# Gated delta rule: the next sequence's loading as steps of the second group's iteration, and the gate products ordered behind their neighbours on TensorE

## The chip, the cores and the metric

The kernel runs on one core of a Trainium2 chip. A core has a matrix engine (TensorE, PE in the profile; PEld is its loading of weights), a vector engine (VectorE, DVE), an engine for functions of one argument (ScalarE, ACT), a general engine (GpSimd, POOL) and one that issues transfers (SyncE, SP). Each works through a queue of its own, and they wait for one another by semaphores. The metric is the time of one execution on the device, in microseconds (us). The median of three runs before the change is 3416.7 us, from 3410.42 to 3425.55.

## The reference

The reference is a stack of four layers on 8 sequences of 512 tokens with 256 features, all in float32: a linear recurrence with an MLP, a mixture of experts, a gated delta rule, and attention over half of the tokens. The change touches the third layer. For each of 8 heads it computes

```python
beta = sigmoid(x @ Wb) * 2
g = -exp(A_log) * softplus(x @ Wa + dt_bias);  alpha = exp(g)
q = l2norm(silu(conv(x @ Wq)));  k = l2norm(silu(conv(x @ Wk)));  v = silu(conv(x @ Wv))

def step(state, inp):                      # over the tokens, state is 64 x 128 for a head
    retained = state @ k_t
    state = a_t * (state - b_t * outer(retained, k_t)) + b_t * outer(v_t, k_t)
    return state, state @ q_t

out = out * rsqrt(mean(out * out) + eps) * o_norm_w * silu(x @ Wg)
return out @ Wo
```

Its `x` is the layer norm of the sum of what came before, and its result is added to that sum. The sum includes the two experts' rows of each token, which lie in a buffer in memory in another order and are gathered when the sequence is loaded.

## The kernel before

`delta_rule` (from L566) takes a sequence's 512 tokens as 4 chunks of 128, and its 8 heads as 2 groups of 4. The recurrence inside a chunk is a triangular system, so that a chunk costs a few products and the inverse of a triangular matrix for each head. The loop at L1071 runs over 16 iterations `n`: sequence `n // 2`, group `n % 2`. An even `n` is called the first group's iteration here, an odd one the second group's.

The work of an iteration is written as generators, each step of which ends in a `yield`:

- `load` (L1016): brings a sequence's `x` in, gathers the rows of its experts eight times with POOL into two buffers `yg` and adds each with DVE (L1031, L1034), then normalises (`center`, L104, result `cz`), transposes (`turn`, L117: eight transposes into two PSUM banks `pc`, two copies by ACT into `cxT`), and calls `decays` (L632: products `pab` with `Wa` and `Wb`, a chain of small steps with Sigmoid, Exp and Ln on ACT, products `pdec`).
- `channels` (L671): the products `pc` for q, k and v, the convolution as one ACT copy and three DVE steps `cy` (L683, L685), Silu (L686).
- `norms` (L689) and `fade` (L721): the lengths of q and k, and the decays between the tokens of a chunk (`pe`, `e`).
- `prepare` (L736): the products `pk` of keys and queries inside a chunk, and from them `NQ`. It is the next group's.
- `inverses` (L751): the inverses for all 16 chunks and heads of the next group: `own` and `low` rearrange `NQ`, DVE inverts blocks of 16 (L789 to L817), and PE joins blocks of 16, 32 and 64 (`pn4`, `pd4`, `pu4`, `pn5` and so on), with ACT copying between the steps (`half`, `NQ`).
- `sides` (L896): transposes `ptv`, `ptk`. `silus` (L918): the gates' products `pg` (L924) and their Silu.
- `advance` (L930): the recurrence over the 4 chunks. From the second chunk on it goes `pkq` (PE, with the state), `old` and `r` (DVE, L952, L953), `pw` (PE), `w` (ACT, L959), `pst` (PE), `state` (DVE, L972), and beside it `pow` and the output `o`.
- `outputs` (L984): squares `oq`, their sum, the gates, transposes `pto`, products `py`, the addition to `x`, and after the second group the store.

The string `order` (L1059) says in which order the steps are written, one letter to a step. It isn't the order on the engines: a scheduler takes the traced instructions, and issues on each engine those that it reckons to be ready, with the written order as priority and the tiles' buffers as a limit. PSUM tiles come from four pools of two banks each: `pc` (`channels` and `turn`), `pa` (`decays`, `norms`, `fade`, `prepare`, `inverses`), `pt_` (`sides`, `silus`, `outputs`) and `pq` (`advance`). So a product can be issued early when its inputs are there and a bank is free. The lines that say when a sequence is loaded:

```python
if n + 2 < total:
    if n % 2 == 0:
        work["l"] = load(n // 2 + 1)
for k in order:
    if k in "cne" and n + 2 < total and k not in work:
        if "l" in work:
            drain(work["l"])
```

The channels of group `n + 2` need the loading, which is finished there whatever is left of it.

Of the kernel before, what the change touches and what calls it, by code (L numbers as in the profile page):

```python
# [14 lines left out]
F32 = mybir.dt.float32  # L15
# [5 lines left out]
P = 128  # L21
B, T, D = 8, 512, 256
NT = T // P
# [22 lines left out]
def block(ctx: ExitStack, tc: tile.TileContext, a: dict, out: bass.AP):  # L46
    nc = tc.nc
    V, S, G, TE = nc.vector, nc.scalar, nc.gpsimd, nc.tensor
# [68 lines left out]
    def turn(pool, tag, src, dst, n, weight=None):  # L117

        for c in range(DK):
            pt = pool.tile([P, T], F32, name=f"pt{n}_{c}", tag=tag)  # L120
            for t in range(NT):
                TE.transpose(pt[:, t * P : (t + 1) * P], src[:, t, c * P : (c + 1) * P], ident)
            if weight is None:
                S.copy(dst[:, c, :], pt)  # L124
            else:
                S.activation(dst[:, c, :], pt, AF.Copy, scale=weight[:, c : c + 1])
# [437 lines left out]


    def delta_rule():  # L566
        with ExitStack() as cx:
            wp = cx.enter_context(tc.tile_pool(name="c_w", bufs=1))
            wq = wp.tile([P, DK, H1 * P], F32, name="wq")
# [50 lines left out]
            tk = cx.enter_context(tc.tile_pool(name="c_tk", bufs=1))  # L620
# [3 lines left out]
            iv = cx.enter_context(tc.tile_pool(name="c_iv", bufs=1))  # L624
# [7 lines left out]
            def decays(b, xT):  # L632

                def s3(tag):
                    return sm.tile([P, NT, H1], F32, name=f"{tag}{b}", tag=tag, bufs=1 if tag.startswith("sp_") else 2)

                pab = pa.tile([P, NT, 2 * H1], F32, name=f"pab{b}", tag="pa")
                for t in range(NT):  # L640
                    for k in range(DK):
                        TE.matmul(pab[:, t, :], xT[:, k, t * P : (t + 1) * P], wab[:, k, :], start=k == 0, stop=k == DK - 1)
                beta = s3("beta")
                S.activation(beta, pab[:, :, H1:], AF.Sigmoid)
                V.tensor_scalar(beta, beta, 2.0, None, ALU.mult)


                y, e, u, l, d = s3("sp_y"), s3("sp_e"), s3("sp_u"), s3("sp_l"), s3("sp_d")
                V.tensor_add(y, pab[:, :, 0:H1], bc(dtb, 1, NT))
                V.scalar_tensor_tensor(e, y, -1.0, y, ALU.mult, ALU.max)  # L650
                S.activation(e, e, AF.Exp, scale=-1.0)
                V.tensor_scalar(u, e, 1.0, None, ALU.add)
                S.activation(l, u, AF.Ln)
                V.tensor_scalar(u, u, -1.0, None, ALU.add)
                V.tensor_scalar(d, u, 0.0, None, ALU.is_equal)
                V.tensor_add(u, u, d)
                V.tensor_add(l, l, d)
# [78 lines left out]
            def prepare(s):  # L736

                b, hg, kq = s.b, s.hg, s.kq
                NQ = s.NQ = hd.tile([P, 2, NU, P], F32, name=f"NQ{b}_{hg}", tag="NQ")
                for t in range(NT):  # L740
                    ts = slice(t * P, (t + 1) * P)
                    e = s.es[t]
                    for h in range(0, HG, 2):
                        pk = pa.tile([P, 2, 2, P], F32, name=f"pk{b}_{hg}_{t}_{h}", tag="pa")
                        for j in range(2):
                            TE.matmul(pk[:, j, :, :], kq[:, h + j, 0, ts], kq[:, h + j, :, ts], start=True, stop=True)  # L746
                        for j in range(2):
                            V.scalar_tensor_tensor(NQ[:, :, t * HG + h + j, :], pk[:, j, :, :], s.nbk[:, t, h + j : h + j + 1], bc(e[:, h + j, :], 1, 2), ALU.mult, ALU.mult)  # L748
                        yield

            def inverses(s):  # L751
# [3 lines left out]
                nm, N = f"{s.b}_{s.hg}", s.NQ[:, 0, :, :]  # L755
# [17 lines left out]
                for a_ in range(4):  # L773
                    q = slice(32 * a_, 32 * a_ + 32)
                    o = own[q, :, :].rearrange("p j (h n) -> p j h n", h=2)
# [3 lines left out]
                V.scalar_tensor_tensor(L[:, 0:256].rearrange("p (r c) -> p r c", c=16), low[:, :, 0:16], front, low[:, :, 16:32], ALU.mult, ALU.add)  # L779
                yield  # L780

                def tmp(what, shape, bufs=2):
                    n = math.prod(shape)
                    t = iv.tile([P, 512], F32, name=f"{what}{nm}", tag="tmp", bufs=bufs)[:, 0:n]
                    names = "abc"[: len(shape)]
                    return t.rearrange(f"p ({' '.join(names)}) -> p {' '.join(names)}", **dict(zip(names, shape)))

# [228 lines left out]
            def load(b):  # L1016

                q = SimpleNamespace(b=b)
                seqs[b] = q
                x = q.x = tk.tile([P, NT, D], F32, name=f"cx{b}", tag="x", bufs=2)  # L1020
                nc.sync.dma_start(x, rows_of(xbufs[0][b]))
                late = []
                for t in range(NT):
                    for j in range(2):
                        at = b * NT + t
                        yg = un.tile([P, D], F32, name=f"yg{b}_{t}_{j}", tag="yg", bufs=2)
                        G.indirect_dma_start(yg, None, ybuf, bass.IndirectOffsetOnAxis(ap=rows[j][:, at : at + 1], axis=0))  # L1027
                        late.append((t, yg, wts[j][:, at : at + 1]))
                        if len(late) > 1:
                            u, y, w = late.pop(0)  # L1030
                            V.scalar_tensor_tensor(x[:, u, :], y, w, x[:, u, :], ALU.mult, ALU.add)  # L1031
                        yield
                for u, y, w in late:
                    V.scalar_tensor_tensor(x[:, u, :], y, w, x[:, u, :], ALU.mult, ALU.add)  # L1034
                yield
                z = tk.tile([P, NT, D], F32, name=f"cz{b}", tag="z")
                center(sm, x, z, f"c{b}")
                yield
                q.xT = tk.tile([P, DK, T], F32, name=f"cxT{b}", tag="xT", bufs=2)
                turn(pc, "pc", z, q.xT, f"c{b}")  # L1040
                q.g, q.beta, q.dec = decays(b, q.xT)
                yield

# [5 lines left out]
            def drain(*work):  # L1049
                for w in work:  # L1050
                    for _ in w:
                        pass
# [2 lines left out]

            order = """  # L1059
                p v p v p l a v p l a v p l a l p a l p a l p a l p l a i a l l g a i l l c g i a a e i a g i e c i a a i e g e  # L1060
                i o c i o c o i c o i c i o o c i i c o i i c o n o n c c n
            """.split()
            groups = {}
            drain(load(0))
            total = B * (H1 // HG)
            for n in range(2):
                s = groups[n] = group(n)
                drain(channels(s), norms(s), fade(s))
                if n == 0:
                    drain(prepare(s), inverses(s))  # L1070
            for n in range(total):  # L1071
                s, s1 = groups.pop(n), groups.get(n + 1)
                work = {"v": sides(s), "g": silus(s), "a": advance(s), "o": outputs(s)}
                if s1 is not None:
                    work |= {"p": prepare(s1), "i": inverses(s1)}
                if n + 2 < total:
                    if n % 2 == 0:
                        work["l"] = load(n // 2 + 1)
                for k in order:
                    if k in "cne" and n + 2 < total and k not in work:  # L1080
                        if "l" in work:
                            drain(work["l"])
                        if n + 2 not in groups:
                            groups[n + 2] = group(n + 2)
                        work[k] = {"c": channels, "n": norms, "e": fade}[k](groups[n + 2])
                    if k in work:
                        next(work[k], None)
                drain(*work.values())

    delta_rule()  # L1090


# [292 lines left out]
```

## Time and profile before

| | |
|---|---|
| median of three runs | 3416.7 us |
| the profiled execution, its own time | 3412.4 us |
| its span, first to last instruction | 3410.6 us |
| PE / DVE / ACT / POOL busy | 89% / 55% / 45% / 19% |
| mean granted clock of TensorE | 0.912 |
| delta rule, first to last transposition or addition of `cx` | about 1544 to 2940 us |

The profile is of one execution. A line of a timeline has the start, the length, the engine, the line of the kernel, the operation, what is written and read, how many instructions stand together, and in brackets the idle time before it and who ended it. A float32 product counts as two PE instructions. The ends of products are modelled. A line of waits has who waited for whom, the total, how often, and the longest. The granted clock is TensorE's share of full speed: at 0.5 a product takes twice as long and still counts as busy.

### The profile page before, as it was taken

What the parts mean: (1) busy time and instruction counts of PE and PEld (TensorE: products, weight loads), DVE (VectorE), ACT (ScalarE), POOL (GpSimd) and SP (SyncE); (2) the same over time, 40 slices, a digit from 0 to 9 for tenths busy, and PEclk for the clock granted to TensorE, in tenths of its full rate; (3) what the DMA queues carried; (4) which work ended last, traced back from release to release, by engine and by line L of the source; (5) the groups of instructions that cost most, each with busy time, mean ns of one, the idle gap of its engine ahead of it and who ended that gap; (6) DMA issues with size and microseconds to landing.
All of it is one profiled execution on the core that took longest, in us unless ns stands there. A gap on an engine that the chain in (4) does not pass through costs nothing. (4 is left out here: it accounts for less than half of the span.)

```text
span 3410.6 us, 59501 instructions
## 1 busy us (share of the span) xinstructions
PE 3049.4 (89%) x24662; PEld 2239.6 (66%) x24662; DVE 1871.4 (55%) x4375; ACT 1528.4 (45%) x2735; POOL 636.5 (19%) x669
## 2 busy tenths in 40 slices
PE   7999999889999999977898999999999998488887
PEld 3655655445999999973666666666666667366564
DVE  4555545334555555546466666666666665554432
ACT  3554442112333333335465757575756565233322
POOL 1000003441011000113131313132222220112111
PEclk8999998999999999998788989899989898687787
DMA  5000003210688888870000000000000000201111
GB/s 204 13 25 13 13 13 147 68 66 19 247 332 329 336 326 318 330 278 20 2 2 26 2 26 2 26 2 26 2 26 2 23 2 8 87 28 38 38 41 47
DMA packets 97133, 302.69 MB, mean 89 GB/s; under 512 B 12760, under 2 KB 79456, under 8 KB 87648
## 3 DMA queue, kind: packets, MB, share of 16 engines
q0 software_dynamic: 19440, 221.19, 17.3%
q1 hardware_dynamic: 68016, 68.44, 6.0%
q10 hardware_dynamic: 9408, 9.27, 0.8%
q8 instruction: 194, 3.18, 0.4%
q14 instruction: 75, 0.61, 0.1%
HBM read 248.79 MB, written 50.08 MB: 88 GB/s over the span
## 5 line engine op out<-in xcount | busy, mean ns | idle before, releaser
L444 PE MATMUL p_r<-zT,w 128*128 128x128 f32 x4544 | 532.8, 275 | 6.8 <-DMA w<-in_experts,wrow 5.6
L444 PEld LDWEIGHTS p_r<-zT,w 128*128 128x128 f32 x4544 | 525.0, 192 | 12.1 <-issue 6.7
L685 DVE SCALAR_TENSOR_TENSOR cy<-pc,conv,cy 128x511 f32<-128x511 f32 (+2 forms) x480 | 353.0, 741 | 99.0 <-ACT cy L683 93.9
L448 ACT ACTIVATE t_r<-p_r,w 128x128 f32<-128x128 f32 x568 | 171.0, 374 | 262.9 <-PE p_r L444 175.8
L444 PE MATMUL p_s<-sxT,shared_w 128*128 128x512 f32 x512 | 224.1, 598 | 1.7 <-ACT sxT L124 1.7
L444 PEld LDWEIGHTS p_s<-sxT,shared_w 128*128 128x128 f32 x512 | 97.4, 192 | 122.6 <-issue 109.2
L449 DVE SCALAR_TENSOR_TENSOR l_r<-p_r,w,t_r 128x128 f32<-128x128 f32 x284 | 80.0, 344 | 175.6 <-PE p_r L444 175.6
L508 POOL DMA_INDIRECT w<-in_experts,wrow x71 | 66.9, 943 | 576.9 <-ACT sg_r L457 565.6
L681 PE MATMUL pc<-cxT,wk 128*128 128x512 f32 x256 | 153.0, 715 | 11.0 <-DVE cy L685 7.6
L681 PE MATMUL pc<-cxT,wq 128*128 128x512 f32 x256 | 147.5, 692 | 6.7 <-DVE cy L685 4.2
L304 PE MATMUL pp<-hT,win 128*128 128x512 f32 x320 | 143.1, 599 | 0.1
L522 PE MATMUL pyr<-w,htr 128*128 128x256 f32 x568 | 135.3, 381 | 2.9 <-DVE htr L462 2.9
L449 DVE SCALAR_TENSOR_TENSOR g_r<-p_r,w,t_r 128x128 f32<-128x128 f32 x284 | 80.0, 345 | 98.1 <-PE p_r L444 98.1
L683 ACT ACTIVATE cy<-pc,conv 128x512 f32<-128x512 f32 x160 | 108.5, 685 | 52.1 <-PE pc L681 51.2
L748 DVE SCALAR_TENSOR_TENSOR NQ<-pk,nbk,e 128x256 f32<-128x256 f32 x256 | 108.8, 478 | 31.6 <-PE pk L746 30.6
L746 PE MATMUL pk<-kq 128*128 128x256 f32 x512 | 125.7, 384 | 0.4 <-DVE NQ L748 0.4
L1027 POOL DMA_INDIRECT yg<-ybuf,rows x64 | 63.2, 987 | 314.6 <-DVE cx L1031 281.7
L394 PE MATMUL pf<-hT,fc 128*128 128x512 f32 x256 | 121.6, 602 | 0.0
L457 ACT ACTIVATE sg_r<-g_r 128x512 f32<-128x512 f32 x71 | 44.8, 630 | 160.1 <-DVE g_r L455 160.1
L399 PE MATMUL pj<-pj,sT 128*128 128x256 f32 x512 | 113.1, 379 | 0.0
L522 PEld LDWEIGHTS pyr<-w,htr 128*128 128x128 f32 x568 | 102.8, 191 | 14.3 <-issue 2.7
L950 PEld LDWEIGHTS pkq<-state,kq 128*128 128x128 f32 x768 | 103.9, 212 | 6.1 <-issue 3.3
(393 smaller groups left out, 6226.9 us busy)
## 6 DMA issues: line engine op xcount, KB each, us to landing
zt<-zbuf SPq DMA_DIRECT2D x71, 128.0 KB
ybuf<-yt SPq DMA_DIRECT2D x71, 128.0 KB, 3.2
zbuf<-zeros SPq DMA_DIRECT2D x11, 768.0 KB, 10.7
x<-in_x SPq DMA_DIRECT2D x8, 512.0 KB
xbuf<-x SPq DMA_DIRECT2D x8, 512.0 KB, 2.9
sx<-xbuf SPq DMA_DIRECT2D x8, 512.0 KB, 4.0
xbuf<-sx SPq DMA_DIRECT2D x8, 512.0 KB, 2.9
cx<-xbuf SPq DMA_DIRECT2D x8, 512.0 KB, 3.8
```

Source lines behind the costliest of these rows:

```text
L304: TE.matmul(ps, win[:, k, m : m + P], hT[:, k, :], start=k == 0, stop=k == DK - 1)
L394: TE.matmul(ps, fc[:, k, f * P : (f + 1) * P], hT2[:, k, :], start=k == 0, stop=k == DK - 1)
L399: TE.matmul(ps, sT[:, f, t * P : (t + 1) * P], pj[:, f, :], start=f == 0, stop=f == 7)
L444: last_of[0] = TE.matmul(ps[:, f, :], wx[:, k, (f0 + f) * P : (f0 + f + 1) * P], xin[:, k, :], start=k == 0, stop=k == DK - 1)
L448: S.activation(t3[:, f, :], p3[:, f, :], AF.Identity, bias=b3[:, f0 + f : f0 + f + 1])
L449: V.scalar_tensor_tensor(t1[:, f, :], p1[:, f, :], b1[:, f0 + f : f0 + f + 1], t3[:, f, :], ALU.add, ALU.mult)
L522: last_of[0] = TE.matmul(ps, hT[:, f, :], w2[:, f, :], start=f == 0, stop=f == 3)
L681: TE.matmul(ps, w[:, k, n * P : (n + 1) * P], xT[:, k, :], start=k == 0, stop=k == DK - 1)
L683: S.activation(y, ps, AF.Copy, scale=conv[:, at + n, 3:4])
L685: V.scalar_tensor_tensor(y[:, j:], ps[:, : T - j], conv[:, at + n, 3 - j : 4 - j], y[:, j:], ALU.mult, ALU.add)
L746: TE.matmul(pk[:, j, :, :], kq[:, h + j, 0, ts], kq[:, h + j, :, ts], start=True, stop=True)
L748: V.scalar_tensor_tensor(NQ[:, :, t * HG + h + j, :], pk[:, j, :, :], s.nbk[:, t, h + j : h + j + 1], bc(e[:, h + j, :], 1, 2), ALU.mult, ...
```

## The change

The loading starts one iteration earlier, as work of the second group's iteration, in ten steps (`l`): eight gathers, the last addition, and `center`. The last two steps (`t`), `turn` and `decays`, which are now separate, follow early in the first group's iteration after it. Ten steps of sequence 1 are done ahead of the loop. For that `x` gets three buffers for two, and `cz` takes the buffer of `oq` (tag `oq`) for one of its own. The order string is rewritten round these letters. And the gates' products are put behind the last product written before them: `Queue` keeps the last TensorE instruction that `delta_rule` writes itself, and `tc.issue_after` adds an order on the same engine, without a wait for completion. `turn` lies outside and goes on with the engine itself. In `tmp` (L782) a parameter that nobody set is dropped.

```diff
+        class Queue:
+            def matmul(self, *args, **kw):
+                self.last = nc.tensor.matmul(*args, **kw)
+            def transpose(self, *args, **kw):
+                self.last = nc.tensor.transpose(*args, **kw)
+        TE = Queue()
...
-                x = q.x = tk.tile([P, NT, D], F32, name=f"cx{b}", tag="x", bufs=2)
+                x = q.x = tk.tile([P, NT, D], F32, name=f"cx{b}", tag="x", bufs=3)
...
-                z = tk.tile([P, NT, D], F32, name=f"cz{b}", tag="z")
+                z = tk.tile([P, NT, D], F32, name=f"cz{b}", tag="oq")
                 center(sm, x, z, f"c{b}")
                 yield
                 q.xT = tk.tile([P, DK, T], F32, name=f"cxT{b}", tag="xT", bufs=2)
                 turn(pc, "pc", z, q.xT, f"c{b}")
+                yield
                 q.g, q.beta, q.dec = decays(b, q.xT)
                 yield
...
             order = """
-                p v p v p l a v p l a v p l a l p a l p a l p a l p l a i a l l g a i l l c g i a a e i a g i e c i a a i e g e
-                i o c i o c o i c o i c i o o c i i c o i i c o n o n c c n
+                p v t p v p l a v p t l a v p a p a p l a p a p a i l a i g a i c l g i a a e i l a g i e c i a a i l e g e
+                i c o i l c o c i o c i l c o i o c i o l i c o i i c o n o n c c n
             """.split()
...
+            coming = load(1)
+            for _ in range(10):
+                next(coming)
             for n in range(total):
...
-                if n + 2 < total:
-                    if n % 2 == 0:
-                        work["l"] = load(n // 2 + 1)
+                if n % 2 == 0 and coming is not None:
+                    work["t"] = coming
+                elif n + 3 < total:
+                    work["l"] = coming = load(n // 2 + 2)
+                else:
+                    coming = None
                 for k in order:
                     if k in "cne" and n + 2 < total and k not in work:
-                        if "l" in work:
-                            drain(work["l"])
+                        if "t" in work:
+                            drain(work["t"])
...
-                    if k in work:
+                    if k == "g":
+                        with tc.issue_after(TE.last.ins):
+                            next(work[k], None)
+                    elif k in work:
                         next(work[k], None)
+                work.pop("l", None)
                 drain(*work.values())
```

More of the change, by code (lines that the diff above doesn't have):

```diff
@@ L780, in inverses, with tmp @@
                 yield
-                def tmp(what, shape, bufs=2):
+                def tmp(what, shape):
                     n = math.prod(shape)
-                    t = iv.tile([P, 512], F32, name=f"{what}{nm}", tag="tmp", bufs=bufs)[:, 0:n]
+                    t = iv.tile([P, 512], F32, name=f"{what}{nm}", tag="tmp")[:, 0:n]
                     names = "abc"[: len(shape)]
```

## The prediction

> **What bounds the kernel now.** I read the page first. TensorE (PE) is busy 89% and is the last engine to wait almost everywhere; the chain that ended last covers under 1% of the span and says nothing here. The change touches the delta rule only, from about 1540 to 2940 us.
>
> ```profile
> PE 3049.4 (89%) x24662; PEld 2239.6 (66%) x24662; DVE 1871.4 (55%) x4375; ACT 1528.4 (45%) x2735; POOL 636.5 (19%) x669
> ```
>
> Next the stretches from one first `pw` product to the next: one per iteration, a sequence's first head group (long), then its second (short). After the length come the busy time and count of PE, PEld, DVE, ACT and POOL, then the granted clock.
>
> ```profile
> 1993.50:2087.90 94.40, 84.88 (x937) 60.30 (x935) 60.29 (x141) 57.66 (x87) 23.57 (x24) 0.89 0.07 20
> 2087.90:2160.70 72.80, 69.11 (x877) 50.42 (x874) 51.23 (x105) 49.23 (x74) 16.58 (x16) 0.95 0.02 6
> ...
> 2327.80:2419.00 91.20, 81.70 (x937) 57.80 (x935) 60.51 (x141) 57.80 (x87) 23.73 (x24) 0.93 0.07 21
> 2491.80:2591.70 99.90, 87.54 (x936) 61.65 (x934) 60.91 (x141) 57.96 (x87) 23.47 (x24) 0.86 0.07 19
> ...
> sum 1010.20, PE 926.88 PEld 664.43 DVE 669.93 ACT 642.10 POOL 239.72; mean PE 77.24 PEld 55.37 DVE 55.83 ACT 53.51 POOL 19.98
> ```
>
> Six sequences take 1010.2, so 168.4 each. Sequence 2 takes 167.2: PE idle 9.5 + 3.7 = 13.2, busy 154.0. The clock column shows 94.4 x 0.11 + 72.8 x 0.05 = 14 us of clock withheld, some 2 of it in idle time, so about 12 of the busy time is slow clock and 142 is work at full clock. The waits of PE over these six sequences name the idle time:
>
> ```profile
> PE pw L957 <- DVE r L953: 23.7, 6, 4.2
> PE pd L837 <- ACT oms L994: 16.1, 6, 2.7
> PE pow L976 <- ACT w L959: 7.6, 12, 0.8
> ```
>
> One wait of some 4 us and one of 2.7 per sequence. Their price is larger than their length. PE's timeline round the first:
>
> ```profile
> 2015.27 1.89 PE L950 MATMUL pkq<-state,kq 128*128 128x64 f32 x16
> 2021.22 1.86 PE L957 MATMUL pw<-r,NQ 128*128 128x64 f32 x8 [4.05 <-DVE r L953]
> ...
> 2027.07 3.62 PE L950 MATMUL pkq<-state,kq 128*128 128x64 f32 x16
> ```
>
> The same `pkq` takes 1.89 before and 3.62 after: stretches of 3.4 us show a clock of 0.50 from 2023.6 to 2040.6. DVE's timeline tells why `r` was late; adds of the load that wait for a gather, and the inverse's transpose, stand ahead of `old` and `r`:
>
> ```profile
> 2015.58 0.48 DVE L1031 SCALAR_TENSOR_TENSOR cx<-yg,wts,cx 128x256 f32<-128x256 f32 x1 [1.86 <-DMA yg<-ybuf,rows]
> ...
> 2017.28 0.71 DVE L763 STREAM_TRANSPOSE low<-own 128x512 f32<-128x512 f32 x1 [0.48 <-ACT own L776]
> ...
> 2019.11 0.68 DVE L952 TENSOR_TENSOR old<-pkq,dec 128x512 f32<-128x512 f32 x1
> 2020.25 0.49 DVE L1034 SCALAR_TENSOR_TENSOR cx<-yg,wts,cx 128x256 f32<-128x256 f32 x1 [0.46 <-DMA yg<-ybuf,rows]
> 2020.65 0.42 DVE L953 TENSOR_TENSOR r<-r,old 128x256 f32<-128x256 f32 x1
> ```
>
> Last, ACT's switches between function tables (count, total, mean ns):
>
> ```profile
> L686 ACT ACT_TABLE_LOAD x6 | 7.7, 1283 | 3.5 <-issue 2.8 <-DVE cy L685 0.7
> L731 ACT ACT_TABLE_LOAD x5 | 6.4, 1283 | 0.1
> ```
>
> **What the Trainium skill says.** "TensorE: Matmul & The Clock Gate", Part 1: a window of about 3.4 us without work halves PE's clock, and a busy window restores it. The trace agrees on 0.50, but a gap of 2.68 us, less than a window, is enough here. "ScalarE: Activation LUTs", What ACT_TABLE_LOAD costs: 1283 ns and a drain of 1380. The 1283 is in the rows; of the drain I see nothing, since after the load that ends at 2052.71 `dec` starts at 2052.73. "Perfetto Trace Analysis", Tensor Engine Instruction: DVE, ACT and POOL are strict FIFO. The DVE lines show it: `old` needs no gather and waits behind one.
>
> **The change part by part.** No computing instruction goes or comes; orders and waits do. I use the orders in which both built programs stand, and walk them with the durations above.
>
> *Loading.* As written, it spreads over the second group's iteration. As ordered, it doesn't: with a third `x` the scheduler draws the eight gathers and adds back into the first group's recurrence, one sequence further ahead. What leaves the recurrence is `center`'s last step (4 x 0.40 of DVE), the eight transposes (1.92 at half clock) and two copies (1.07 of ACT) of `turn`; they stand at the second group's end, 1.0 of PE at full clock. The gathers land 2.8 us after issue; about 7 us of DVE work lies between the add that frees a buffer and the next use, so I price their waits at 0.3 a sequence. If that cover goes, `old` and `r` wait again as now, up to 4 us. On SP, the load of `x` waits for the store of three sequences before, which ends in the same iteration as today's; store and load land in 2.9 and 3.8, and the first add comes some 8 us later. Nothing. The scheduler's choice is thus already a part of the claim that fails.
>
> *`cz` in `oq`'s buffer.* It waits for the reduction of `oq` (1.2) that precedes it in DVE's order; the next `oq` comes a whole recurrence later. Nothing on PE; but four `cz` (1.6) now delay the gates in the second group: about 1 us late for `pto`.
>
> *`pg` after its written neighbour.* Two tiles (4 products, 1.7 us) stand between the second `pkq` and `pw`, two round the third. DVE needs 0.68 + 0.41 there: the 4.05 is covered, if nothing else is ahead. The edge is order alone; gates are read only after the recurrence.
>
> *`decays` as a step of its own, early.* `pab` now precedes the first `pkq` and the first `pc` products become filler. Its chain of Sigmoid, Exp and Ln took from 2038.2 to 2050.3; now it runs inside the recurrence. At step 1, `r` stands behind one more `cy` (0.68 + 0.74 + 0.41 = 1.8 against one `pc` of 0.86): 1.0 idle. The Ln load (1.28) holds a DVE step and `state` behind it: 0.8. Also `pab` and `pdec` take the two `pa` banks, so the last products of `prepare` come after `pdec`, and the inverse chain starts one recurrence step late.
>
> *What is late next.* From the end of the last `pkq` DVE needs `old` 0.68, `L` 0.64, `r` 0.41, seven small rows with statistics 3.9, `o` 0.42, four steps 1.04 + 0.69 + 1.08 + 0.68, `both` 0.68, then `cols` 0.61 on ACT and `dn` 0.71: about 11. PE has 7 queued before `pn4`: 4.1 idle. Then `half` waits behind `oq` 1.04, two copies 1.4, a Sqrt load 1.28, `rsc` and `oms`: 3.5. Sequences 2, 4, 6 come so. Sequences 1, 3, 5 stand in another order: 19 loads in the first group's iteration (13 before), 7 in the second's (10 before). There `w` of step 1 waits for the Ln load (1.6) and the tail for six more loads, 7.7 us; I make its idle time 10.4.
>
> Sum, even sequences: 142 work + 1.0 + 0.8 + 0.3 + 4.1 + 3.5 + 2.9 (two `half`-fed waits after) + slow clock over some 12 us, 4, + second group 2.4 idle and 2 slow = 163. Odd: 142 + 0.3 + 1.6 + 10.4 + 1.5 + 8 slow + 1.9 = 165.7. Mean 164.4 against 168.4: 4.0 less. The first and last sequences have parts of it, so 6.5 x 4.0 = 26. The profiled execution of 3412.4 becomes 3386. It lies 4.3 below the median of 3416.7; on that scale I say 3391.
>
> **Unknown sizes.** Slow clock: none at all would save 5 more a sequence, and lasting to the iteration's end costs 5. Tail waits: from 0 if ACT gets ahead of its queue, to 18 if every load lands on the path. A gain is possible too, since filler hides late inputs.
>
> **Rivals.** (1) *The late inverse sets the end: slower.* One step of the recurrence is about 10 us, and all of it may be exposed between the last `pow` and `pn5`. For: DVE and ACT are in order, and the filler has been moved ahead. Against: `pc` tiles can still be interleaved. My sums have 9 of idle time there; break-even is 13 (9 + 4.0), and at 18.5 a sequence takes 5.5 more than now: 3416.7 + 36 = 3453. (2) *PE stays at full clock: much faster.* For: 12 us of slow clock a sequence come from two waits that both get filler. If the tail waits halve too, a sequence takes 154: 6.5 x 14.4 = 94, so 3323. Against: the tail has no filler left. (3) *An exchange:* the wait at `pw` reappears at `pn4` at the same price, 3400 to 3434. For: the same work on DVE and ACT must precede it.
>
> **How the numbers follow.** Forecast 0.36 (own range 3370 to 3400), rival 1 0.26, rival 2 0.18, rival 3 0.20. About 0.5%, 17 us, is what a measurement tells here. Faster takes the forecast and rival 2: 0.54; rival 3 is the same, 0.20; slower 0.26. Rival 2 covers 3300 to 3365 and rival 1 3434 to 3480; the range 3328 to 3462 leaves out the outer parts of both, 0.09 and 0.08.
>
> **What would show it.** Right: `pw` no longer waits 4 us for `r`; `pn` of the first inverse product waits for `dn` by 3 to 5 us in first-group iterations, and `pn5` for `half`; the half clock moves from the recurrence to the tail; odd sequences are longer in the first group; 20 and 26 table loads a sequence against 23. Wrong: waits for gathers on DVE ahead of `old` again, clock at 0.5 in the recurrence, or tail waits over 13 us.

## The result and the profile after

The changed kernel takes 3392.1 us (median of 4 runs, 3391.5 to 3397.4) against 3421.1 for the kernel before on the same chip (four runs, of which the prediction's 3416.7 is the median of three): a ratio of 0.992, with a 95% interval of 0.989 to 0.995. It is faster by 0.8%. The profiled execution took 3392.6 us with a span of 3390.8, and the one before 3412.4 with 3410.6.

First the line of busy times, where ACT's count has gone from 2735 to 2745, all of them table loads:

```profile
PE 3014.9 (89%) x24662; PEld 2225.2 (66%) x24662; DVE 1896.5 (56%) x4375; ACT 1541.7 (45%) x2745; POOL 632.6 (19%) x669
```

Next the stretches from one first `pw` to the next, as before the change (length, busy time and count of PE, PEld, DVE, ACT, POOL, then granted clock): sequence 2 with its two groups, sequence 3 with its two, and the six sequences from 1 to 6 together:

```profile
2002.90:2092.70 89.80, 79.43 (x933) 58.00 (x932) 64.03 (x141) 58.60 (x87) 25.17 (x24) 0.92 0.06 19
2092.70:2162.00 69.30, 67.61 (x894) 49.62 (x893) 53.35 (x109) 46.95 (x73) 16.44 (x16) 1.00 0.04 12
2162.00:2256.20 94.20, 80.10 (x916) 58.50 (x915) 62.80 (x136) 63.93 (x90) 23.66 (x24) 0.86 0.05 16
2256.20:2329.90 73.70, 68.25 (x878) 49.35 (x877) 52.44 (x105) 45.03 (x70) 15.50 (x16) 0.95 0.03 8
1837.70:2815.60 977.90, 882.28 (x10815) 645.01 (x10814) 687.81 (x1439) 645.71 (x959) 229.52 (x230) 0.92 0.04 12
```

A sequence takes 163.0 on average (977.9 / 6) and took 168.4. Two forms alternate: sequences 2, 4 and 6 take 159.1, 160.7 and 157.7, sequences 1, 3 and 5 take 165.2, 167.9 and 167.3. The waits of PE over the same six sequences (who waited for whom, total, times, longest):

```profile
PE pn L571 <- ACT e L741: 21.2, 4, 6.0
PE pu L571 <- issue: 14.4, 10, 2.4
PE pn L571 <- DVE dn L773: 6.9, 2, 3.7
...
PE pw L571 <- DVE inv L804: 6.2, 2, 3.1
PE pw L571 <- DVE r L963: 5.8, 13, 0.9
```

The wait of `pw` for `r`, 4.2 at its longest before, is at most 0.9. In its place `pn`, the first product of the inverses (`pn4`), waits up to 6.0. The waits of `pu` named "issue" are 14.4 in all, 4.0 before; the profile shows nothing that ended them, and what they are is open. Most of the half clock has moved to the tail too, but not all: in sequences 1, 3 and 5 it is 0.50 for 3.4 to 6.8 us in the second recurrence step, after a wait of 1.37 of `pst` for `w`. PE's timeline from the last `pw` of sequence 2's first group into its tail, and the product `pn4` in sequence 3:

```profile
2044.76 1.07 PE L571 MATMUL pw<-r,NQ 128*128 128x64 f32 x8 [3.12 <-DVE inv L804]
...
2055.13 1.32 PE L571 MATMUL pn<-dn,NQ 32*32 32x16 f32 x128 [3.67 <-DVE dn L773]
...
2062.70 0.49 PE L571 MATMUL pn<-half,NQ 32*32 32x32 f32 x8 [1.51 <-ACT half L849]
2063.13 2.07 PE L571 MATMUL pc<-cxT,wq 128*128 128x512 f32 x2
```

```profile
2214.72 1.91 PE L571 MATMUL pn<-dn,NQ 32*32 32x16 f32 x128 [5.98 <-ACT e L741]
```

Two `pc` instructions take 2.07 in sequence 2's tail, where four took 1.94 at full clock just before (at 2049.53). In sequence 3 `dn` was written by 2213.50; the wait's last 1.2 us are for ACT's `e`, which reads `pe` in one of the two `pa` banks and had come behind a table load (1.28).

Where the time went, then. The first `pw` of the delta rule comes at 1670.0 and came at 1662.5; sequence 0 takes 167.7 and took 163.0; sequences 1 to 6 are 32.3 shorter together; what follows takes 575.2 (3390.8 - 2815.6) and took 574.9. 7.5 + 4.7 - 32.3 + 0.3 = -19.8, the difference of the spans.

### The profile page after: what moved, and what is told of

Read it like the earlier page. It is cut to its first block, busy times and chain, and to the rows that moved or that the text cites. A ratio compares the mean times of both kernels' runs of the same rounds, so it can differ in the third digit from the quotient of the medians.

```text
span 3390.8 us, 59551 instructions
## 1 busy us (share of the span) xinstructions
PE 3014.9 (89%) x24662; PEld 2225.2 (66%) x24662; DVE 1896.5 (56%) x4375; ACT 1541.7 (45%) x2745; POOL 632.6 (19%) x669
## 5 line engine op out<-in xcount | busy, mean ns | idle before, releaser
L444 PEld LDWEIGHTS p_r<-zT,w 128*128 128x128 f32 x4544 | 526.9, 192 | 11.8 <-issue 6.1
L695 DVE SCALAR_TENSOR_TENSOR cy<-pc,conv,cy 128x509 f32<-128x509 f32 (+2 forms) x480 | 351.4, 740 | 120.9 <-ACT cy L693 116.1
L571 PE MATMUL pc<-cxT,wq 128*128 128x512 f32 x256 | 143.8, 682 | 14.4 <-DVE cy L695 10.9
L571 PE MATMUL pc<-cxT,wk 128*128 128x512 f32 x256 | 143.6, 654 | 7.2 <-DVE sp_l L669 3.3
L738 POOL TENSOR_TENSOR e<-le,g 128x512 f32<-128x512 f32 x64 | 68.3, 1073 | 351.9 <-DVE NQ L758 314.6
```

The costliest lines, as they stand in the source:

```text
L444: last_of[0] = TE.matmul(ps[:, f, :], wx[:, k, (f0 + f) * P : (f0 + f + 1) * P], xin[:, k, :], start=k == 0, stop=k == DK - 1)
L571: self.last = nc.tensor.matmul(*args, **kw)
L695: V.scalar_tensor_tensor(y[:, j:], ps[:, : T - j], conv[:, at + n, 3 - j : 4 - j], y[:, j:], ALU.mult, ALU.add)
L738: G.tensor_mul(e, bc(le, 1, HG), bc(s.g[:, t, hs], 2, P))
```

## The experiments

All times below are per sequence from sequence 1 to 6, first `pw` to first `pw`, in the profiled execution; the ratio is that of the medians to the kernel before on the same chip. Idle is PE's time without work. "Half" is PE's busy time in stretches whose granted clock is 0.5, so half of it is lost; "work" is the rest, the busy time less half of "half".

| kernel | median us | ratio (95%) | a sequence | idle | half | work |
|---|---|---|---|---|---|---|
| before | 3421.1 | 1 | 168.4 | 13.9 | 26.2 | 141.4 |
| changed | 3392.1 | 0.992 (0.989 to 0.995) | 163.0 | 15.9 | 18.2 | 137.9 |
| e1 edge alone | 3458.9 | 1.014 (1.009 to 1.019) | 175.1 | 16.3 | 37.2 | 140.2 |
| e2 no edge | 3391.6 | 0.993 (0.991 to 0.996) | 161.2 | 15.3 | 17.5 | 137.1 |
| e3 sequence 1 written later | 3406.5 | 0.997 (0.995 to 0.999) | 162.0 | 16.1 | 16.3 | 137.7 |
| e4 decays in other banks | 3397.9 | 0.994 (0.992 to 0.995) | 164.2 | 12.8 | 23.2 | 139.9 |
| e5 sequence 2 held | 3391.7 | 0.992 (0.989 to 0.994) | 162.4 | 15.1 | 18.2 | 138.2 |
| e6 as e4, `pdec` later | 3337.4 | 0.975 (0.972 to 0.978) | 154.8 | 10.1 | 13.5 | 137.9 |
| e7 before, no gathers | 3380.4 | 0.988 (0.985 to 0.992) | 167.2 | 11.8 | 30.7 | 140.0 |
| e8 decays late | 3339.2 | 0.977 (0.974 to 0.980) | 153.4 | 8.8 | 10.6 | 139.3 |
| e9 as e8, no edge | 3372.6 | 0.985 (0.982 to 0.989) | 160.3 | 12.1 | 20.1 | 138.1 |
| e10 as e8, sequence 2 held | 3337.2 | 0.975 (0.971 to 0.978) | 153.7 | 9.8 | 9.3 | 139.2 |
| e11 as e8, channels held | 3422.6 | 1.003 (1.001 to 1.004) | 168.3 | 12.0 | 33.4 | 139.7 |
| e12 as e8, no gathers | 3290.2 | 0.963 (0.958 to 0.968) | 149.8 | 6.8 | 7.6 | 139.2 |

The work is 137 to 141 in all fourteen, so what differs is idle time and slow clock. The spread of 4 in that column says how finely this division can be read.

### The two halves of the change apart: e1 and e2

e1 is the kernel before with `Queue` and the edge only:

```diff
+                    if k == "g":
+                        with tc.issue_after(TE.last.ins):
+                            next(work[k], None)
-                    if k in work:
+                    elif k in work:
```

> The kernel before with only the gates' products queued behind the last product written before them; loading, order string and buffers stay. Theory (the loading's place and the early decays make the gain, the edge itself little): the adds of the gathers still stand ahead of `old` and `r` on DVE in the third recurrence step, so `pw` still waits some 4 us for `r`, the half clock after it stays, a sequence stays at 168 +- 1.5, the time within 0.5% of before. Rival (the gates' products are what fills the wait): `pw` waits under 1.5 us there, a sequence takes 163 to 165, the time is 20 to 30 us below before. In the order of this kernel as built only `pk` stands between that `pkq` and `pw`, and the gates' products come later, which speaks for the first.

e2 is the changed kernel without those three lines:

> The changed kernel without the edge on the gates' products: loading a sequence ahead, decays early, new order string, third x. Theory: the gain is here, all of it, 20 to 32 us below before, and `pw` has no wait of 4 us for `r`. As built its sequences all have one order, not two, so the tail should wait alike in all of them, some 4 to 6 us before `pn4`. Rival (the edge is needed for the gain): within 10 us of before, with a wait of 3 us or more at `pw` in the recurrence.

The edge alone makes the kernel 1.4% slower, which neither theory had. e1's longest wait of PE over its six sequences, and one that is new:

```profile
PE pw L571 <- DVE r L963: 23.2, 12, 4.1
...
PE pdec L571 <- DVE g L673: 11.7, 6, 2.7
```

The wait of `pw` is as long as before, and a wait of `pdec` (2.7) and one of `pd` for ACT's `up` (11.4 in all, 2.6 at most) have joined it. Why the edge does that in the old order was not taken apart further. e2 gives all of the gain: 161.2 a sequence, in one form for all of them, and no wait of `pw` for `r`. Its tail waits more than expected:

```profile
PE pn L571 <- DVE dn L773: 45.9, 6, 8.5
```

That is 7.6 a sequence, and it shows where the changed kernel is short. As built, e2 too has gate tiles and `pc` between the first and second `pkq` and their `pw`, without any edge.

### The early decays: e4, e6 and e8

e4 takes decays' two PSUM tiles from the banks of `advance`:

```diff
-                pab = pa.tile([P, NT, 2 * H1], F32, name=f"pab{b}", tag="pa")
+                pab = pq.tile([P, NT, 2 * H1], F32, name=f"pab{b}", tag="pq")
...
-                ps = pa.tile([P, 3, NT, H1], F32, name=f"pdec{b}", tag="pa")
+                ps = pq.tile([P, 3, NT, H1], F32, name=f"pdec{b}", tag="pq")
```

> The changed kernel with the two PSUM tiles of decays, `pab` and `pdec`, taken from the two banks of advance and not from the two that prepare and inverses use. Theory (these tiles make the last `pk` and with them the inverses one recurrence step late, and that is what PE waits for in the tail of a first group): the waits of 4 to 6 us before `pn4` and the half clock after them go, a sequence takes 155 to 159 against 163, and the time is 25 to 45 us below the changed kernel. Rival (ACT's table loads and the small DVE steps ahead of `dn` are late whatever the banks): `pn` still waits 3 us or more in the tail, a sequence takes 161 to 165, the time within 12 us of the changed kernel. A loss is possible too: `pab` in the banks of `pkq` and `pw` may hold the recurrence's first step by 2 to 3 us a sequence, 15 to 20 us in all.

e6 is e4 with `pdec` one recurrence step later and queued behind that step's `pkq`:

```diff
+                yield
                 ps = pq.tile([P, 3, NT, H1], F32, name=f"pdec{b}", tag="pq")
+                with tc.issue_after(TE.last.ins):
-                for n, m in enumerate((le, gt, ones)):
-                    TE.matmul(ps[:, n, :, :], m, g, start=True, stop=True)
+                    for n, m in enumerate((le, gt, ones)):
+                        TE.matmul(ps[:, n, :, :], m, g, start=True, stop=True)
...
-  ... a p a p a i l a i g a i c l g ...
+  ... a p a p a i l a t i g a i c l g ...
```

> As the kernel with both tiles of decays in advance's banks, but the products `pdec` are written one recurrence step later and queued on TensorE behind that step's `pkq`. There the waits before `pn4` had gone and a wait of `pdec` for `g`, 4.1 us a sequence, with half clock behind it, had come; a sequence took 164. Theory (a wait on TensorE costs its length and about as much again in slow clock): no wait of `pdec` over 0.5 us, a sequence takes 155 to 159, the time is 30 to 50 us below the changed kernel. Rival (the work ahead of `pn4` or of `pn5` on DVE and ACT is what is short, and every wait taken away comes back at the next place): some other wait of 3 us or more in the first group's iteration, 161 to 165 a sequence, within 12 us of the changed kernel.

e8 is the changed kernel with the step of decays moved back to where it stood in the kernel before, ahead of the first channels, its banks untouched:

```diff
-  ... p l a v p t l a v p a p a p l a p a p a i l a i g a i c l g ...
+  ... p l a v p l a v p a p a p l a p a p a i l a i g a i t c l g ...
```

> The changed kernel with decays as a step of its own but written late, just ahead of the first channels, as in the kernel before; its tiles are in the same two banks as there. As built `pk` is all issued by the first recurrence step, `pab` in the second and `pdec` behind the last `pow`. Theory (early decays take the banks and make the inverses late): no wait of `pn4` over 2 us; the chain of decays' small steps ends at the tail instead, where `pdec` and `pe` may wait 2 to 3 us for `g`; 160 to 164 a sequence, within 12 us of the changed kernel. Rival (the inverses are late by DVE's and ACT's own work): `pn` waits 3 us or more for `dn` or `e` here too, and a sequence takes 163 to 167.

e4's waits of PE over its six sequences have `pn` no more among the long ones, but `pdec`:

```profile
PE pdec L571 <- DVE g L673: 24.6, 6, 4.1
```

The edit changes the banks alone, and the tail's wait went; but the scheduler moved much more than the two tiles: ACT's count fell to 2697, and all that went are table loads (15 to 17 a sequence, 21 to 25 in the changed kernel). So e4 alone can't tell the banks from the table loads, which its rival named; e8, with 20 to 22 loads (below), has no long wait of `pn` either, which speaks for the late inverse. The time stayed, as the rival had it, because `pdec`, ahead of `pst` in PE's queue, now waits 4.1, with 0.50 behind it (half 23.2 against 18.2). e6 takes that wait away, and a sequence falls from 164.2 to 154.8; five of its sequences take 153.8 to 159.6 and the last 143.6. It is not free of waits: `pn` still waits for `dn` 14.6 in all, 3.1 at most, which was the rival's sign; the time was the theory's.

e8 gets 153.4 by another way, without touching a bank. `pk` stands ahead of the second `pw` again and ends by 2002.9; in the changed kernel's sequence 2 it runs until 2034.9. All six sequences together:

```profile
1836.70:2757.10 920.40, 867.67 (x10815) 623.96 (x10814) 684.77 (x1439) 633.01 (x948) 237.70 (x230) 0.96 0.04 13
```

Its longest waits are these, none over 2.5; `pn` waits for `dn` 3.4 in all, 1.9 at most:

```profile
PE pdec L571 <- DVE g L673: 13.3, 6, 2.5
PE pc L571 <- DVE cy L695: 9.7, 6, 1.9
```

The theory had the waits right; its 160 to 164 a sequence was 7 too high. The early decays, a part of the change, thus cost 9.6 a sequence (163.0 - 153.4), with the late inverse and all else that comes with their place; the rest of the change is worth 15.0 (168.4 - 153.4). Both e6 and e8 beat the kernel before and the changed one.

### What the earlier loading buys: e7, e11 and e12

The prediction held the additions that wait for gathers to be the cause of the wait of 4 us. e7 takes gathers and additions out of the kernel before, and leaves the experts' part out of the layer's input:

```diff
                     for j in range(2):
+                        yield
+                        continue
                         at = b * NT + t
```

> The kernel before without the gathers and their additions: the experts' part is left out of x in the third layer. Theory (as in the prediction: `old` and `r` are late in the third recurrence step because additions that wait for gathers stand ahead of them on DVE): the wait of 4 us of `pw` for `r` and the half clock after it go, 6 to 10 us a sequence, 40 to 65 us in all. Rival (`r` is late behind `low`, `cy` and the other work, the gathers are only what is seen): `pw` still waits 3 us or more, less than 3 us a sequence.

Both were half right. e7's waits, and PE's timeline between that `pkq` and its `pw`:

```profile
PE pc L681 <- DVE cy L685: 18.3, 12, 2.0
PE pc L681 <- DVE sp_d L655: 11.5, 6, 2.4
...
PE pw L957 <- DVE r L953: 4.2, 6, 0.7
```

```profile
1989.33 0.99 PE L122 MATMUL ptc<-ident,cz 128*128 128x128 f32 x6
1990.16 1.03 PE L924 MATMUL pg<-wg,cxT 128*128 128x256 f32 x4
1991.89 1.08 PE L957 MATMUL pw<-r,NQ 128*128 128x64 f32 x8 [0.71 <-DVE r L953]
```

The wait of `pw` is all but gone, 23.7 to 4.2, for two reasons. `r` ends 2.25 after the end of that `pkq` and no longer 3.8 (means of the six), so the gathers and additions account for some 1.6 of the wait; and the scheduler has put transposes and gate products there, which cover 1.7 more. But a sequence is only 1.2 shorter. The slow clock stays: 0.50 begins 27.5 to 28.3 us after a sequence's first `pw`, where it began before (25.2 to 28.0), though the wait ahead of it is now 0.7, and the time at half clock rises from 26.2 to 30.7. `pc` waits after that, for `sp_d` and `cy`. Most of e7's gain is at the start: its first `pw` comes at 1645.6 (before 1662.5) and sequence 0 takes 154.7 (before 163.0).

e11 asks about filler. It is e8 with the channels' products held as the gates' are:

```diff
-                    if k == "g":
+                    if k == "g" or k == "c" and k in work:
```

> The kernel with decays late, and the channels' products queued behind the last product written before them, from their second step on. As built no `pc` stands in the recurrence before the last `pw`; there is no `pc` between the second and third `pkq` and their `pw`, and one or two gate tiles. Theory (what the earlier loading buys is `pc` as filler for DVE's and ACT's steps in the recurrence): 160 to 168 a sequence as in the kernel before, with waits of `pw` for `r`, of `pst` for `w` and of `pkq` for `state` of 1 to 3 us in each step, and half clock. Rival (it buys that gathers no longer stand ahead of `old` and `r`): 153 to 157 a sequence.

A sequence takes 168.3, as before the change. e11's longest waits, then the `pab` products ahead of its slow clock in sequence 2, and the stretches (columns as before) on both sides of its onset:

```profile
PE pto L574 <- DVE gate L1007: 18.7, 9, 3.1
PE pw L571 <- DVE sp_l L670: 11.0, 5, 2.2
```

```profile
2014.78 1.91 PE L571 MATMUL pab<-wab,cxT 128*128 128x16 f32 x16
```

```profile
2015.20:2018.70 3.50, 3.50 (x34) 3.50 (x33) 0.72 (x3) 3.37 (x5) 2.52 (x3) 0.99 0.02 5
2018.70:2042.60 23.90, 21.18 (x80) 17.76 (x80) 16.66 (x49) 7.99 (x12) 11.59 (x12) 0.50 0.10 27
```

The idle time grows by 3.2 only, from 8.8 to 12.0; the time at half clock triples, 10.6 to 33.4, which costs 11.4. Most of that slow clock follows no wait. In each of the six sequences 0.50 begins 13.7 to 16.0 us after the first `pw` and lasts 23.9 to 30.7 us, while PE is shown as all but fully busy in the 6.8 us before. In e8 `pc` products (128x512) stand after the same `pab` and between `pow` and `pkq`, and its clock stays full until 34.7 us or later. So with `pc` kept out of the recurrence the gain of 15 is gone. The theory's number all but came true, its mechanism did not: the waits of `pw` for `r` are 4.1 in all, and `r` ends 1.7 to 1.9 us after its `pkq` on average in each step (1.2 to 1.8 in e8, 4.3 and 3.8 in the first two before the change). By these figures `pc` keeps the clock there more than it covers waits. Why the clock falls without it is not shown, and how much of the 15 the edge on `pc` costs by itself, with later waits at the last `pw` and at `pto`, is open.

e12 is e8 without gathers and additions, with the same order of products in the recurrence of the first group (a few change places later); it too leaves the experts' part out:

> The kernel with decays late without the gathers and their additions: the experts' part is left out of x in the third layer. The order of the products is the same as with them. Theory (loaded a sequence ahead, the gathers cost the recurrence 0.3 us a sequence, and their cost is in the start alone): 152.5 to 155 a sequence, and 15 to 25 us less at the first `pw`. Rival (the additions still hold DVE's queue): 148 to 151 a sequence.

149.8, nearer to the rival; the first `pw` comes 20.4 earlier, as the theory had it. The gathers and additions cost 3.6 a sequence in e8, but not by holding `old` and `r`: `r` ends 1.8, 1.2 and 1.4 after its `pkq` in the three steps of a first group, with them and without. The last section tells of one place. e12 also has 20 table loads a sequence for 22, and no run takes the two apart.

### The edge again, with decays late: e9

e9 is e8 without the edge.

> The kernel with decays late, without the edge on the gates' products. As built two `pg` tiles then stand at the second and third `pw` and `pc` starts one recurrence step later; the rest of the order is alike. Theory (with decays late there is filler enough either way; the edge is worth nothing by itself): within 12 us of the kernel with decays late, 152 to 156 a sequence, `pw` waits under 1 us for `r`. Rival (the edge keeps `pc` early and the tail free): 158 to 165 a sequence, 25 us or more above it.

The rival was right: 160.3, so the edge is worth 6.9 a sequence here, where it was worth -1.8 with early decays (161.2 without it, 163.0 with) and -6.7 in the old order. Without it `pc` starts a step later and gate tiles fill the recurrence; `pow` then waits for `w` (8.7 in all), `pdec` for `g` (16.9), and "half" is 20.1 against 10.6. Table loads rise as well, from 22 to 27 a sequence in sequences 1 to 5. So the edge has no fixed value; it depends on the order around it, and by which of these ways was not tested.

### The start: e3, e5 and e10

e3 writes sequence 1's ten steps into the first iteration:

```diff
-            for _ in range(10):
-                next(coming)
...
+                    if n == 0:
+                        work["l"] = coming
```

> The changed kernel, but sequence 1's ten steps of loading are written as steps of the first iteration and not ahead of the loop. Between the start of the delta rule and the first `pw` of sequence 1 the changed kernel takes 12 us more than before. Theory (the ten steps put gathers and adds of sequence 1 ahead of sequence 0's channels and norms on DVE): 8 to 12 us less than the changed kernel, the first `pw` of sequence 1 at 1826 to 1830, periods of the later sequences unchanged. Rival (the loss comes from the early decays or the products' order): less than 3 us of difference, the wait of 9 us of `pn` for `dn` stays.

A miss for both: the first `pw` came at 1672.4 and that of sequence 1 at 1844.2, and the start got no shorter. POOL's timeline of the changed kernel shows what else was there, the last gathers ahead of the first `e`; below it that stretch of the kernel before:

```profile
1561.76 0.94 POOL L1037 DMA_INDIRECT yg<-ybuf,rows  x1 [3.40 <-DVE sp_u L666]
...
1584.48 0.94 POOL L1037 DMA_INDIRECT yg<-ybuf,rows  x1 [0.33 <-DVE cx L1044]
1600.75 1.27 POOL L742 TENSOR_TENSOR e<-e,le 128x512 f32<-128x512 f32 x1 [15.33 <-ACT e L741]
```

```profile
1561.21 0.94 POOL L1027 DMA_INDIRECT yg<-ybuf,rows  x1 [3.29 <-DVE sp_u L656]
...
1593.78 1.26 POOL L732 TENSOR_TENSOR e<-e,le 128x512 f32<-128x512 f32 x1 [24.99 <-ACT e L731]
```

Counted from the first gather, 26 stand ahead of that `e`, in e3 as well, and 18 in the kernel before. With a third `x` the scheduler takes sequence 2's loading into the start, wherever sequence 1's is written. e5 holds sequence 2's steps:

```diff
+                    elif k == "l" and n == 1 and k in work:
+                        with tc.issue_after(hold["at"][0].ins), tc.issue_after(hold["at"][1].ins):
+                            next(work[k], None)
```

(`hold["at"]` is sequence 0's `r` and `state` of the second recurrence step, on DVE and POOL.)

> The changed kernel, with sequence 2's gathers and additions put behind sequence 0's second recurrence step on GpSimd and VectorE. In the changed kernel, and in the one whose sequence 1 was written later, the trace shows 24 gathers ahead of sequence 0's fade where the kernel before has 16: the third x lets the scheduler draw sequence 2 into the start. Theory (that costs the start 7 us before the first `pw`, and some of the loss after it): the first `pw` comes at 1661 to 1664 and not 1670, the time is 5 to 10 us below the changed kernel. Rival (the start is longer for another reason): the first `pw` at 1668 to 1672, or the loss only moves into sequence 0's recurrence and the time stays within 4 us.

16 gathers stand ahead, and the first `pw` comes at 1662.8, as in the kernel before. But sequence 0 then takes 173.0, so the first `pw` of sequence 1 is at 1835.8 against 1837.7, and the medians are the same. e10 does it with decays late:

> The kernel with decays late, and sequence 2's gathers and additions behind sequence 0's second recurrence step. In the kernel with decays late the first `pw` of the delta rule comes at 1666.6 and sequence 0 takes 170 us, where later ones take 153 to 155. Theory (the start's loss is the third sequence's loading in the prologue): first `pw` at 1659 to 1662, 5 to 10 us less than the kernel with decays late. Rival (the loss moves into sequence 0's recurrence, as it did in the changed kernel): sequence 0 takes 175 or more and the time is within 4 us.

Its first `pw` is at 1668.2, which looks like a miss, but its delta rule began 7 us later: from the first transposition to the first `pw` it is 117.8, in e8 123.5, in the kernel before 117.8. Sequence 0 takes 168.7 against 170.1. The theory held for the start, and the gain of some 6 us is too small to be told by medians of 3337.2 and 3339.2 from two chips. What makes sequence 0 take 15 us more than a later one in e8 is open.

## Why the prediction was right, point by point

**The time.** 3391 was forecast and 3392.1 measured. That they lie so near is luck: two terms of the sum were wrong and cancelled in part, to 19.8 of gain in the profiled execution where 26 were forecast, and the 4.3 added for the median hid most of the rest, for the profiled execution after lies within 0.5 of its median. The step that failed is "the first and last sequences have parts of it, so 6.5 x 4.0 = 26". A sequence gained 5.4, not 4.0, and the start and sequence 0 lost 12.2 instead of gaining. I had priced the third `x` in the steady state only and not asked what the scheduler does with a free buffer at the start; e5 and e10 show that what it draws in costs 6 to 7 us up to the first `pw`. In e5 that loss comes back in sequence 0, so what makes the 12.2 as a whole is open.

**Even sequences: 163 said, 159.2 measured.** `pn4`'s wait is 3.67 (4.1 said). `pn5`'s is 1.51 (3.5 said), the 2.9 after it didn't come, and one wait was not foreseen, 3.12 of the last `pw`: on DVE `r` stood behind a copy of two columns that took 2.51 while POOL was at work (the last section shows it). Idle time in sequence 2 is 12.1 against 15.0 in my sum, slow clock 11.3 / 2 = 5.7 against 6, work 141.4 against 142. So the mis-sized term is the tail's.

**Odd sequences: 165.7 said, 166.8 measured.** The wait of `w` at step 1 is 1.37 (1.6 said); `pn4` waits 5.98. Idle time in sequence 3 is 19.6 against 15.7, slow clock 24.6 / 2 = 12.3 against 8. Table loads are 21 in sequences 2 and 4 and 25 in 1, 3 and 5 (20 and 26 said), but they are not what makes the odd tail long, as I had it: of the 5.98 one load's delay of 1.2 is theirs, and by the lines 3.2 is a meeting of DVE and POOL told in the last section. I had no term for that. It does not set the odd sequences apart from the even ones either, which lose as much by such meetings (2.4, 0.6 and 0.2 ahead of `dn` in sequence 2) and pay at `pw` and `pn4`. What sequence 3 has beyond sequence 2 are smaller waits, of `pst` 1.37, `pow` 1.01, `pu` 1.39 and 2.42 and `pkq` 1.95, and more slow clock.

**The banks.** "`pab` and `pdec` take the two `pa` banks, so the inverse chain starts one recurrence step late" was right, and the heaviest sentence of the prediction: e4 removes the wait with other banks (and fewer table loads), e8 with another time and as many loads. I had put it down as a cost inside a gain and did not add up that the early decays take back two thirds of the gain, 9.6 of 15.0.

**The price of the 4 us wait.** Here the reading failed in part. That its length and the slow clock behind it could be won was wrong for the old order: in e7 the wait is down to 0.7 and a sequence wins 1.2, because 0.50 begins at the same place all the same and the products behind it wait later. So the wait of 4 us was not what the slow clock hung on alone; what else it hung on is not shown.

**The gates' products.** "The 4.05 is covered" by two `pg` tiles: the tiles do stand there, but e2 has filler there without the edge, and e1 has the edge with the wait still at 4.1. I credited the edge with what the rest of the change does.

**The gathers' 0.3.** DVE's waits for gathers over the six sequences are 3.4, so 0.6 each (5.9 in all before). As a wait that was small, as said, if twice the 0.3; as a cost it was not, for gathers and additions together are 3.6 in e8, by e12.

**Rivals.** Rival 2's "a sequence takes 154" is reached by e8 (153.4), with decays late rather than by the change. Rival 1's mechanism, the late inverse, is there and costs 9.6 a sequence, with the rest of what early decays bring, which the 15.0 of the other parts outweigh. A window without work, which the Trainium skill gives as the condition for half clock ("TensorE: Matmul & The Clock Gate", Part 1), isn't needed in this case: the wait of 2.5 in e8 is followed by a stretch at 0.50, and in e11 0.50 follows 6.8 us that are shown as all but fully busy.

## What to carry to other kernels

Split a change into parts before judging it: here one part was worth 15 us a sequence and another took 9.6 back, and an edge was worth 7, -2 or -7 by what stood round it. When TensorE waits at one place, ask what independent products could stand there and from when they are available; taking away one wait gave 1.2 us, the earlier loading with its `pc` as filler 15. Look at the clock as well as at the waits: it fell where PE was shown busy, and a product at 0.50 is lost time that no list of waits shows. And a PSUM tile that is moved early holds its bank early: look at whose products share it, and at what a spare buffer lets a scheduler do at the start.

## What was unexpected in the hardware

Some of DVE's small steps that work on SBUF alone take far longer when POOL works at the same time. In the tail of sequence 3 of the changed kernel two small steps of the inverse take 2.00 and 1.67. DVE's timeline, and POOL's of the same stretch:

```profile
2203.11 2.00 DVE L803 TENSOR_TENSOR p<-L,inv 128x32 f32<-128x32 f32 x1
...
2205.37 1.67 DVE L803 TENSOR_TENSOR p<-L,inv 128x50 f32<-128x50 f32 x1
```

```profile
2202.76 0.95 POOL L1037 DMA_INDIRECT yg<-ybuf,rows  x1 [1.16 <-DVE mvc L110]
2203.72 1.28 POOL L742 TENSOR_TENSOR e<-e,le 128x512 f32<-128x512 f32 x1
2204.94 0.76 POOL L1000 TENSOR_TENSOR gate<-gate,o 128x256 f32<-128x256 f32 x1
2205.68 1.25 POOL L742 TENSOR_TENSOR e<-e,le 128x512 f32<-128x512 f32 x1
```

Over the delta rule of the changed kernel 58 of these `p` steps meet no POOL instruction and take at most 0.33 (mean 0.24); 38 meet one and take up to 2.01 (mean 0.82). The sums `inv<-p` between them take at most 0.25 beside POOL and 0.26 without it. In sequences 1 and 3 the two make the inverse 2.00 + 1.67 - 0.46 = 3.2 us later (0.46 is what the two take alone). Sequence 5 is in the same order and meets POOL in one such step (1.21); its `pn4` waits 4.68 for 5.98. In sequences 2 and 4 it is a copy of two columns, ahead of the last `r`, and POOL's two multiplications in the same 2.5 us:

```profile
2041.38 2.51 DVE L799 COPY inv<-L 128x2 f32<-128x2 f32 x1
2041.37 2.48 POOL L742 TENSOR_TENSOR e<-e,le 128x512 f32<-128x512 f32 x2
```

In the first groups of e8's sequences 1 to 6 this copy meets no POOL instruction and takes 0.15 or 0.16. So some 2.4 of the last `pw`'s wait of 3.12 lie here. e8 has the same with `both`, two steps of 128 x 256:

```profile
2027.57 4.58 DVE L826 TENSOR_SCALAR both<-inv,front 128x256 f32<-128x256 f32 x1
2032.07 1.36 DVE L827 TENSOR_SCALAR both<-inv,second 128x256 f32<-128x256 f32 x1
```

```profile
2025.04 1.69 POOL L1037 DMA_INDIRECT yg<-ybuf,rows  x1 [0.56 <-DVE sp_l L670]
2026.75 4.02 POOL L738 TENSOR_TENSOR e<-le,g 128x512 f32<-128x512 f32 x4
2030.74 3.81 POOL L742 TENSOR_TENSOR e<-e,le 128x512 f32<-128x512 f32 x3
```

and e12, where no gather stands ahead of the multiplications:

```profile
1996.98 1.02 DVE L826 TENSOR_SCALAR both<-inv,front 128x256 f32<-128x256 f32 x1
1997.92 1.12 DVE L827 TENSOR_SCALAR both<-inv,second 128x256 f32<-128x256 f32 x1
```

In the second groups of both kernels, where POOL does nothing at that moment, each takes 0.35. The pair takes 5.9 here in sequence 2 and 4.7 in e8's sequences 1, 3, 4 and 5, 2.1 in e12's, and `dn`, for which `pn4` waits, is behind it. The Trainium skill describes it ("SBUF — State Buffer", SBUF: two separate sides): DVE and GpSimd share a pair of ports, and where a DVE step has two inputs in SBUF or is in a two-port mode, the one that comes second waits until the other's instruction is through. The rows agree as to the waiting; which mode the copy and `both` are in they do not say. And 4.58 is longer than one multiplication (4.02 / 4 = 1.0), so more than one went ahead, as with the copy. The 4.7 - 2.1 = 2.6 could be most of the 3.6 a sequence between e8 and e12, if all of it reached PE; no run has moved POOL's work alone, so the size of its effect on the time is open.
